# Relational attention with four heads at a time: scores in four row strips, relation sums in four column strips, one set of 8 PSUM banks

## Chip, cores, metric

The kernel runs on one core of one Trainium2 chip. The time is microseconds on the device, the median of several runs (they agree within 0.1%). The profile is one execution seen by the hardware profiler. PE is the matmul engine, PEld its weight loads, DVE, ACT and POOL the other compute engines. A record is one instruction in the profile; an fp32 matmul of the program is two records. The granted clock is the share of PE's full clock that was let through to it. The chain is the work that ended last, followed back from the end of the run. A PSUM bank is one of eight buffers that PE writes its results to. The runs were taken on several chips; the kernel before, run beside each of them, took 7752.3 to 7752.8 us in all of them.

## The reference, cut to what matters

Two layers over 64 graphs of 256 nodes with 256 features, all in fp32. Layer 0 is a graph attention (twice) with a feed-forward. Layer 1 is the one that changes:

```python
q, k: (64, 8 heads, 256, 32)
scores = einsum('bhid,bhjd->bhij', q, k) / sqrt(32)
attn = softmax(scores, axis=-1)
for r in range(4):
    v_r = src @ Wv[r] + bv[r]                      # per head: 256 x 32
    out += einsum('bhij,bhjd->bhid', attn * (adj_matrix == r), v_r)
attn_out = out @ Wo + bo                           # then norm, feed-forward (gelu), norm
```

A head has 32 features: a score matmul fills 32 rows of PE's 128 x 128 array, a relation sum (32 output features, 128 nodes contracted) 32 columns.

## The kernel before

Two graphs are one group, 32 groups follow each other. In a group's attention the heads are worked off one by one, `weighted` two heads ahead of `applied`:

```python
def bank(name):
    return psum.tile([P, 512], F32, tag="g", name=name, bufs=3)
...
def weighted(b, h):                                   # softmax, i on the partitions
    hp = slice(a * DH, (a + 1) * DH)                  # a = h % 4: the head's strip
    ps = psum.tile([P, NB, N], F32, tag="s", bufs=2)
    for i in range(NB):
        nc.tensor.matmul(ps[:, i, :], q[hp, m, i0:i0 + P], k_[hp, m, ...])          # sp
    nc.vector.tensor_reduce(nm[:, 0, :], ps, AX.X, ALU.max)                          # hm
    nc.vector.tensor_scalar(nm[:, 0, :], nm[:, 0, :], -isd, None, op0=ALU.mult)
    for i in range(NB):
        nc.scalar.activation(e[:, i, :], ps[:, i, :], AF.Exp, bias=nm[:, 0, i:i + 1],
                             scale=isd, accum_out=nm[:, 1, i:i + 1])
    nc.vector.reciprocal(nm[:, 2, :], nm[:, 1, :])
    nc.gpsimd.tensor_mul(e, e, ...)

def applied(b, h, e, po):
    pt = psum.tile([P, NB * N], F32, tag="pt", bufs=2)
    ...                                               # 4 transposes of e into pt
    for r in range(NR):                               # the four masks: er
        nc.vector.scalar_tensor_tensor(er[:, r, :], aT[b], float(r), pt,
                                       op0=ALU.is_equal, op1=ALU.mult)
    for r in range(NR):
        for j in range(NB):
            nc.tensor.matmul(po[hp, m, :], v[...head h...], er[:, r, j * N:(j + 1) * N],
                             start=(r == 0 and j == 0), stop=(r == NR - 1 and j == NB - 1))
```

The eight PSUM banks are 3 (general), 2 (scores), 2 (transposes) and 1 (sums). A scheduler fixes each engine's order when the kernel is built.

## Time and profile before

| | before |
|---|---|
| time | 7752.3 us (7750.9 to 7753.7, 4 runs) |
| PE, DVE busy | 85%, 39% of the span |
| one group | 240.6 us, of it the attention loop 98.8 us |

"The loop" is always the stretch from a group's first score matmul to the start of its second output projection; "the rest" is what lies between two loops.

### The profile page before, as it was taken

How to read it: one execution, taken by the hardware profiler on the slowest of the kernel's cores; microseconds unless marked ns; L12 is line 12 of the kernel's file. 1: busy time of each engine (PE TensorE's matmuls, PEld its weight loads, DVE VectorE, ACT ScalarE, POOL GpSimd, SP SyncE). 2: the span in 40 equal slices, each digit the busy share in tenths (PEclk: the TensorE clock that was granted, in tenths of full speed). 3: DMA queues.
4: the chain of work that ended last, by engine and by line, in shares of the span. 5: the costliest groups of instructions: out<-in, count | busy, mean ns of one | idle time of the engine just before them, and what ended most of it. 6: DMA issues, size and time to landing. Idle time of an engine off the chain costs nothing.

```text
span 7751.0 us, 62264 instructions
## 1 busy us (share of the span) xinstructions
PE 6591.3 (85%) x24104; PEld 3643.6 (47%) x24104; DVE 2999.6 (39%) x6544; ACT 1505.7 (19%) x3968; POOL 1417.2 (18%) x1193
## 2 busy tenths in 40 slices
PE   7888888888888888888888888888898888988888
PEld 4444444444444444444444444444444444444444
DVE  3344433344333443334433343433434334343343
ACT  1121122211212112122111221112211122111221
POOL 1111111111111111111111211111111111111111
PEclk8999989999989999899998999989999899998999
DMA  2000000000000000000000000000000000000000
GB/s 61 9 9 6 3 9 9 9 6 3 9 9 9 6 3 9 9 9 6 3 9 8 9 6 3 9 9 9 9 1 9 9 9 9 1 8 9 3 3 3
DMA packets 63094, 62.85 MB, mean 8 GB/s; under 512 B 7248, under 2 KB 62160, under 8 KB 62800
## 3 DMA queue, kind: packets, MB, share of 16 engines
q1 hardware_dynamic: 33792, 33.56, 1.3%
q0 software_dynamic: 16896, 16.78, 0.9%
q10 hardware_dynamic: 12112, 8.54, 0.4%
q8 instruction: 191, 3.13, 0.2%
q14 instruction: 103, 0.84, 0.0%
HBM read 42.09 MB, written 16.78 MB: 8 GB/s over the span
## 4 chain that ended last, share of the span: by engine, by line
PE 67%; issue 13%; DVE 11%; POOL 5%; ACT 3%; ACTq 0%; DMA 0%; POOLq 0%; DVEq 0%
PE po L321 24%; PE sp L292 7%; PE h1p L250 7%; PE yfp L216 6%; PE vp L278 6%; PE pt L313 5%; PE qp L266 2%; PE ygp L216 2%; PE gTp L355 2%; DVE er L317 2%; PE yop L216 2%; POOL rs L232 2%; PE kp L266 1%; DVE s L198 1%; DVE s L199 1%
## 5 line engine op out<-in xcount | busy, mean ns | idle before, releaser
L321 PE MATMUL po<-er,v 128*32 128x256 f32 x8192 | 1923.9, 391 | 154.6 <-DVE er L317 154.6
L317 DVE SCALAR_TENSOR_TENSOR er<-aT,pt 128x512 f32<-128x512 f32 x2048 | 1316.7, 678 | 1181.9 <-PE pt L313 1181.9
L321 PEld LDWEIGHTS po<-er,v 128*32 128x32 f32 x8192 | 783.7, 112 | 1073.9 <-DVE er L317 256.2
L302 POOL TENSOR_TENSOR e<-e,hm 128x512 f32<-128x512 f32 x512 | 531.7, 1041 | 3032.7 <-DVE hm L301 2980.3
L299 ACT ACTIVATE e<-sp,hm 128x256 f32<-128x256 f32 x1024 | 476.0, 470 | 2625.0 <-DVE hm L296 2624.9
L219 DVE TENSOR_TENSOR yf<-yfp,res 128x512 f32<-128x512 f32 x128 | 88.5, 692 | 1770.1 <-PE yfp L216 1770.1
L292 PE MATMUL sp<-k,q 32*128 32x256 f32 x2048 | 649.3, 429 | 67.4 <-ACT e L299 67.4
L250 PE MATMUL h1p<-h1T,wf 128*128 128x512 f32 x1024 | 519.0, 671 | 23.8 <-DVE h1T L153 23.8
L250 PE MATMUL h1p<-h3T,w 128*128 128x512 f32 x1024 | 515.6, 668 | 22.1 <-DVE h3T L153 22.1
L292 PEld LDWEIGHTS sp<-k,q 32*128 32x128 f32 x2048 | 304.0, 189 | 360.2 <-issue 266.6
L216 PE MATMUL yfp<-w,h 128*128 128x256 f32 x2048 | 447.3, 379 | 0.0
L216 PE MATMUL yfp<-wf,h 128*128 128x256 f32 x2048 | 447.2, 379 | 0.0
L278 PE MATMUL vp<-wv,h2T 128*128 128x512 f32 x1024 | 444.7, 592 | 0.0
L313 PE MATMUL pt<-ident,e 128*128 128x128 f32 x2048 | 418.9, 307 | 7.3 <-POOL e L302 6.3
L232 POOL TENSOR_TENSOR rs<-ve,mhalf 128x4 f32<-128x4 f32 x128 | 130.7, 1021 | 1588.3 <-DVE ve L231 1588.3
L216 PEld LDWEIGHTS yfp<-w,h 128*128 128x128 f32 x2048 | 389.1, 190 | 66.6 <-issue 15.3
L216 PEld LDWEIGHTS yfp<-wf,h 128*128 128x128 f32 x2048 | 389.1, 190 | 66.6 <-issue 15.3
L280 DVE TENSOR_TENSOR v<-vp,rbv 128x512 f32<-128x512 f32 x256 | 177.1, 692 | 561.9 <-PE vp L278 561.9
L313 PEld LDWEIGHTS pt<-ident,e 128*128 128x128 f32 x2048 | 223.2, 146 | 325.4 <-issue 271.1
L250 PEld LDWEIGHTS h1p<-h1T,wf 128*128 128x128 f32 x1024 | 219.5, 218 | 306.9 <-issue 256.5
L250 PEld LDWEIGHTS h1p<-h3T,w 128*128 128x128 f32 x1024 | 218.3, 217 | 305.7 <-issue 254.3
L295 DVE TENSOR_REDUCE hm<-sp 128x2 f32<-128x512 f32 x512 | 350.0, 684 | 14.9 <-PE sp L292 11.7
(470 smaller groups left out, 5798.8 us busy)
## 6 DMA issues: line engine op xcount, KB each, us to landing
xs<-in_x_dram SPq DMA_DIRECT2D x32, 512.0 KB, 3.5
af<-in_adj_dram POOLq DMA_DIRECT2D x32, 512.0 KB, 4.2
out_dram<-res SPq DMA_DIRECT2D x32, 512.0 KB, 2.8
wf<-in_L_gnn_w_ff_dram ACTq DMA_DIRECT2D x2, 1024.0 KB, 12.4
w<-in_L_gnn_W_dram ACTq DMA_DIRECT2D x2, 1024.0 KB, 9.9
wv<-in_L_gnn_Wv_dram ACTq DMA_DIRECT2D x4, 256.0 KB, 5.1
rbv<-in_L_gnn_bv_dram ACTq DMA_DIRECT2D x1, 512.0 KB, 6.8
gat1we<-in_L_gnn_W_dram ACTq DMA_DIRECT2D x1, 256.0 KB, 4.2
```

What stands on the lines that cost most here:

```text
L216: nc.tensor.matmul(ps[:, i * F:(i + 1) * F], lhs(t, k), rhs(b, k), start=(k == 0), stop=(k == n - 1))
L232: nc.gpsimd.tensor_tensor(rs, ve, mhalf, ALU.pow)
L250: nc.tensor.matmul(ps, wi[:, k, f * P:(f + 1) * P], hT[:, k, :], start=(k == 0), stop=(k == KB - 1))
L266: nc.tensor.matmul(ps, w[:, k, m * P:(m + 1) * P], hT[:, k, :], start=(k == 0), stop=(k == KB - 1))
L278: nc.tensor.matmul(ps, hT[:, k, t * P:(t + 1) * P], wvf[:, k, cs], start=(k == 0), stop=(k == KB - 1))
L292: nc.tensor.matmul(ps[:, i, :], q[hp, m, i0:i0 + P], k_[hp, m, b * N:(b + 1) * N], start=True, stop=True)
L295: nc.vector.tensor_reduce(nm[:, 0, :], ps, AX.X, ALU.max)
L299: nc.scalar.activation(e[:, i, :], ps[:, i, :], AF.Exp, bias=nm[:, 0, i:i + 1], scale=isd, accum_out=nm[:, 1, i:i + 1])
L302: nc.gpsimd.tensor_mul(e, e, nm[:, 2, :, None].to_broadcast([P, NB, N]))
L313: nc.tensor.transpose(pt[:, j * N + i * P:j * N + (i + 1) * P], e[:, i, j * P:(j + 1) * P], ident)
L317: nc.vector.scalar_tensor_tensor(er[:, r, :], aT[b], float(r), pt, op0=ALU.is_equal, op1=ALU.mult)
L321: nc.tensor.matmul(po[hp, m, :], v[:, b * NB + j, r * F + h * DH:r * F + (h + 1) * DH], er[:, r, j * N:(j + 1) * N], start=(r == 0 and j = ...
```

## The change

The intent: four heads of a feature block (a "quad") lie in four different strips of the array, so if their matmuls alternate, PE can run four at once. The core of the diff:

```diff
-        def weighted(b, h):
-            ps = psum.tile([P, NB, N], F32, tag="s", name=f"sp{n}", bufs=2)
+        def weighted(b, m):
+            ps = [bank(f"sp{n}_{a}") for a in range(HPB)]
             for i in range(NB):
-                nc.tensor.matmul(ps[:, i, :], q[hp, m, i0:i0 + P], ...)
+                for a in range(HPB):
+                    hp = slice(a * DH, (a + 1) * DH)
+                    nc.tensor.matmul(ps[a][:, i * N:(i + 1) * N], q[hp, m, i0:i0 + P], ...)
+            for a in range(HPB):
+                ...                                   # softmax as before, head by head
-        def applied(b, h, e, po):
-            pt = psum.tile([P, NB * N], F32, tag="pt", name=f"pt{n}", bufs=2)
+        def applied(b, m, es, po):
+            for a in range(HPB):
+                pt = bank(f"pt{n}_{a}")
+                ...                                   # transposes and masks, head by head
             for r in range(NR):
                 for j in range(NB):
-                    nc.tensor.matmul(po[hp, m, :], ...)
+                    for a in range(HPB):              # heads innermost
+                        nc.tensor.matmul(po[hp, m, :], ...)
-        ahead = [weighted(*heads[0]), weighted(*heads[1])]
+        ahead = [weighted(*quads[0])]                 # one quad ahead
```

With it, `bank` becomes one set of `bufs=8` for everything; the masks `er` get five buffers (before: two), which the feed-forward's hidden layer, cut in two halves, shares; the exponentials `e` get five (before: three); three other buffers are reduced by one to make room. DVE, ACT and POOL have the same instructions as before.

More of the change, by code (lines that the diff above doesn't have):

```diff
@@ L54, in bank @@
     def bank(name):
-        return psum.tile([P, 512], F32, tag="g", name=name, bufs=3)
+        return psum.tile([P, 512], F32, tag="g", name=name, bufs=8)
     def load(u):
@@ L98, in gat_weights @@
         nc.vector.tensor_copy(ar, ac[:, :, None].to_broadcast([P, 2 * KB, P]))
-        wt = work.tile([P, KB, F], F32, tag="h1", name=f"{name}wt", bufs=1)
+        wt = work.tile([P, KB, F], F32, tag="big", name=f"{name}wt", bufs=5)
         for c in range(KB):
@@ L143, in to_features @@
     def to_features(src, name, scale=None, shift=None):
-        dst = work.tile([P, KB, TN], F32, tag="hT", name=name, bufs=3)
+        dst = work.tile([P, KB, TN], F32, tag="hT", name=name, bufs=2)
         for k in range(KB):
@@ L179, in gat_weighted @@
             nc.tensor.matmul(rows, wa[:, k, :], hT[:, k, :], start=(k == 0), stop=(k == KB - 1))
-        wh = work.tile([P, T, F + 1], F32, tag="wh", name=f"wh{name}")
+        wh = work.tile([P, T, F + 1], F32, tag="wh", name=f"wh{name}", bufs=1)
         for t in range(T):
@@ L186, in gat_weighted @@
             nc.scalar.copy(wh[:, t, :], ps[:, :F + 1])
-        s = work.tile([P, T, N], F32, tag="s", name=f"s{name}")
+        s = work.tile([P, T, N], F32, tag="s", name=f"s{name}", bufs=1)
         for t in range(T):
@@ L245, in feed_forward @@
     def feed_forward(u, l, hT, wi, bi, func, wo_, res):
-        h1 = work.tile([P, FB, TN], F32, tag="h1", name=f"h1{u}_{l}", bufs=1)
+        h1 = [work.tile([P, FB // 2, TN], F32, tag="big", name=f"h1{u}_{l}_{c}", bufs=5)
+              for c in range(2)]
         for f in range(FB):
@@ L251, in feed_forward @@
                                  start=(k == 0), stop=(k == KB - 1))
-            nc.scalar.activation(h1[:, f, :], ps, func, bias=bi[:, f:f + 1])
+            nc.scalar.activation(h1[f * 2 // FB][:, f % (FB // 2), :], ps, func, bias=bi[:, f:f + 1])
         y = work.tile([P, T, F], F32, tag="y", name=f"yf{u}_{l}")
         for b in range(G):
-            add_blocks(u, f"yfp{l}_", y, res, b, lambda t, k: h1[:, k, t * P:(t + 1) * P],
+            add_blocks(u, f"yfp{l}_", y, res, b, lambda t, k: h1[k * 2 // FB][:, k % (FB // 2), t * P:(t + 1) * P],
                        lambda b, k: wo_[:, k, :], FB)
@@ L282, in attention @@
         isd = 1.0 / math.sqrt(DH)
-        def weighted(b, h):
-            m, a = divmod(h, HPB)
-            hp = slice(a * DH, (a + 1) * DH)
-            n = f"{u}_{b}_{h}"
-            ps = psum.tile([P, NB, N], F32, tag="s", name=f"sp{n}", bufs=2)
+        def weighted(b, m):
+            n = f"{u}_{b}_{m}"
+            ps = [bank(f"sp{n}_{a}") for a in range(HPB)]
             for i in range(NB):
                 i0 = b * N + i * P
-                nc.tensor.matmul(ps[:, i, :], q[hp, m, i0:i0 + P],
-                                 k_[hp, m, b * N:(b + 1) * N], start=True, stop=True)
-            nm = work.tile([P, 3, NB], F32, tag="hm", name=f"hm{n}", bufs=4)
-            nc.vector.tensor_reduce(nm[:, 0, :], ps, AX.X, ALU.max)
-            nc.vector.tensor_scalar(nm[:, 0, :], nm[:, 0, :], -isd, None, op0=ALU.mult)
-            e = work.tile([P, NB, N], F32, tag="e", name=f"e{n}", bufs=3)
-            for i in range(NB):
-                nc.scalar.activation(e[:, i, :], ps[:, i, :], AF.Exp, bias=nm[:, 0, i:i + 1],
-                                     scale=isd, accum_out=nm[:, 1, i:i + 1])
-            nc.vector.reciprocal(nm[:, 2, :], nm[:, 1, :])
-            nc.gpsimd.tensor_mul(e, e, nm[:, 2, :, None].to_broadcast([P, NB, N]))
-            return e
@@ L305, in applied @@
-        def applied(b, h, e, po):
-            m, a = divmod(h, HPB)
-            hp = slice(a * DH, (a + 1) * DH)
-            n = f"{u}_{b}_{h}"
-            pt = psum.tile([P, NB * N], F32, tag="pt", name=f"pt{n}", bufs=2)
-            for j in range(NB):
-                for i in range(NB):
-                    nc.tensor.transpose(pt[:, j * N + i * P:j * N + (i + 1) * P],
-                                        e[:, i, j * P:(j + 1) * P], ident)
-            er = work.tile([P, NR, NB * N], F32, tag="er", name=f"er{n}", bufs=2)
-            for r in range(NR):
-                nc.vector.scalar_tensor_tensor(er[:, r, :], aT[b], float(r), pt,
-                                               op0=ALU.is_equal, op1=ALU.mult)
+                for a in range(HPB):
+                    hp = slice(a * DH, (a + 1) * DH)
+                    nc.tensor.matmul(ps[a][:, i * N:(i + 1) * N], q[hp, m, i0:i0 + P],
+                                     k_[hp, m, b * N:(b + 1) * N], start=True, stop=True)
@@ new lines, in weighted @@
+            nm = work.tile([P, HPB, 3, NB], F32, tag="hm", name=f"hm{n}", bufs=3)
+            es = []
+            for a in range(HPB):
+                pv = ps[a].rearrange("p (i n) -> p i n", i=NB)
+                nc.vector.tensor_reduce(nm[:, a, 0, :], pv, AX.X, ALU.max)
+                nc.vector.tensor_scalar(nm[:, a, 0, :], nm[:, a, 0, :], -isd, None, op0=ALU.mult)
+                e = work.tile([P, NB, N], F32, tag="e", name=f"e{n}_{a}", bufs=5)
+                for i in range(NB):
+                    nc.scalar.activation(e[:, i, :], pv[:, i, :], AF.Exp, bias=nm[:, a, 0, i:i + 1],
+                                         scale=isd, accum_out=nm[:, a, 1, i:i + 1])
+                nc.vector.reciprocal(nm[:, a, 2, :], nm[:, a, 1, :])
+                nc.gpsimd.tensor_mul(e, e, nm[:, a, 2, :, None].to_broadcast([P, NB, N]))
+                es.append(e)
@@ new lines, in weighted @@
+            return es
+        def applied(b, m, es, po):
+            n = f"{u}_{b}_{m}"
+            ers = []
+            for a in range(HPB):
+                pt = bank(f"pt{n}_{a}")
+                for j in range(NB):
+                    for i in range(NB):
+                        nc.tensor.transpose(pt[:, j * N + i * P:j * N + (i + 1) * P],
+                                            es[a][:, i, j * P:(j + 1) * P], ident)
+                er = work.tile([P, NR, NB * N], F32, tag="big", name=f"er{n}_{a}", bufs=5)
+                for r in range(NR):
+                    nc.vector.scalar_tensor_tensor(er[:, r, :], aT[b], float(r), pt,
+                                                   op0=ALU.is_equal, op1=ALU.mult)
+                ers.append(er)
@@ L319, in applied @@
             for r in range(NR):
                 for j in range(NB):
-                    nc.tensor.matmul(po[hp, m, :],
-                                     v[:, b * NB + j, r * F + h * DH:r * F + (h + 1) * DH],
-                                     er[:, r, j * N:(j + 1) * N],
-                                     start=(r == 0 and j == 0),
-                                     stop=(r == NR - 1 and j == NB - 1))
-        heads = [(b, h) for b in range(G) for h in range(H)]
-        ahead = [weighted(*heads[0]), weighted(*heads[1])]
@@ L329, in attention @@
-        for n, (b, h) in enumerate(heads):
-            if h == 0:
-                po = psum.tile([P, KB, N], F32, tag="o", name=f"po{u}_{b}")
-            applied(b, h, ahead.pop(0), po)
-            if n + 2 < len(heads):
-                ahead.append(weighted(*heads[n + 2]))
-            if h == H - 1:
+                    for a in range(HPB):
+                        h = m * HPB + a
+                        hp = slice(a * DH, (a + 1) * DH)
+                        nc.tensor.matmul(po[hp, m, :],
+                                         v[:, b * NB + j, r * F + h * DH:r * F + (h + 1) * DH],
+                                         ers[a][:, r, j * N:(j + 1) * N],
+                                         start=(r == 0 and j == 0),
+                                         stop=(r == NR - 1 and j == NB - 1))
@@ L336, in attention @@
+        quads = [(b, m) for b in range(G) for m in range(KB)]
+        ahead = [weighted(*quads[0])]
+        for n, (b, m) in enumerate(quads):
+            if n + 1 < len(quads):
+                ahead.append(weighted(*quads[n + 1]))
+            if m == 0:
+                po = bank(f"po{u}_{b}").rearrange("p (m n) -> p m n", m=KB)
+            applied(b, m, ahead.pop(0), po)
+            if m == KB - 1:
                 nc.scalar.copy(oT[:, :, b * N:(b + 1) * N], po)
@@ L348, in tile_gat_layer__then__relational_attention_layer @@
         att, whs = gat_weighted(u, 0, hT, gat1, off)
-        hT = work.tile([P, KB, TN], F32, tag="hT", name=f"gT{u}", bufs=3)
+        hT = work.tile([P, KB, TN], F32, tag="hT", name=f"gT{u}", bufs=2)
         for m in range(KB):
```

## The prediction

> **What bounds the kernel now.** I read the page's busy table first (PE 85% of the span, DVE 39%), then the chain that ended last (PE 67%, its largest line the relation sums `po`), then the groups, and then one of the 32 groups of two graphs as a timeline. In the chain the second feed-forward of a group starts at 2416.89 us and that of two groups later at 2898.13 us: 240.6 us a group, and x 32 that is 7700 of the 7751 us. The kernel is 32 equal copies, laid end to end. Inside a group the attention loop runs from the first score matmul at 2310.08 us to the second output projection at 2408.90 us. These are busy times by engine in that stretch, and the chain in it:
>
> ```profile
> 2310.08:2408.90 98.82, 90.67 (x394) 42.29 (x393) 55.08 (x118) 17.45 (x67) 16.61 (x16) 0.97 0.00 1
> ```
>
> The columns are length, then PE, weight load, DVE, ACT and POOL busy, then the granted clock. The loop is 98.8 us, 41% of a group, and PE is busy in 90.7 of it at nearly full clock; DVE in 55.1. The rest of the group (142 us) is not touched by the change except for buffer counts. The groups that the change concerns:
>
> ```profile
> L321 PE MATMUL po<-er,v 128*32 128x256 f32 x8192 | 1923.9, 391 | 154.6 <-DVE er L317 154.6
> L317 DVE SCALAR_TENSOR_TENSOR er<-aT,pt 128x512 f32<-128x512 f32 x2048 | 1316.7, 678 | 1181.9 <-PE pt L313 1181.9
> ...
> L292 PE MATMUL sp<-k,q 32*128 32x256 f32 x2048 | 649.3, 429 | 67.4 <-ACT e L299 67.4
> ...
> L313 PE MATMUL pt<-ident,e 128*128 128x128 f32 x2048 | 418.9, 307 | 7.3 <-POOL e L302 6.3
> ...
> L295 DVE TENSOR_REDUCE hm<-sp 128x2 f32<-128x512 f32 x512 | 350.0, 684 | 14.9 <-PE sp L292 11.7
> ```
>
> The reader is to see that `po` uses 32 of 128 columns and `sp` 32 of 128 rows, that each fp32 matmul of the program is two records (64 graphs x 8 heads x 2 score products make x2048 records, x 8 relation products x8192), and that DVE waited 1181.9 us for the transposes: it follows PE. The means of 391 and 429 ns are latencies of pipelined work; start to start, single records say otherwise: `po` 213 ns (most of its intervals lie at 210 to 219), `sp` 213, `pt` 108. So a loop of 16 heads needs on PE 256 x 0.213 = 54.5 us for `po`, 64 x 0.213 = 13.6 for `sp`, 64 x 0.108 = 6.9 for `pt`: 75 us. The other 24 us are changes between the three shapes (a first record after a change starts 307 ns after the last, against 213: some 0.1 us, five or six times a head, 9 us), the lead-in, and 6.8 us at half clock near the start.
>
> **Do strips overlap?** Already now, where two heads meet by accident:
>
> ```profile
> 2310.08 1.14 PE L292 MATMUL sp<-k,q 32*128 32x256 f32 x8
> ...
> 2377.10 1.93 PE L321 MATMUL po<-er,v 128*32 128x256 f32 x12
> 2378.96 0.69 PE L292 MATMUL sp<-k,q 32*128 32x256 f32 x2
> ```
>
> Eight score records of heads 0 and 1 take 1.14 us; one after the other they would need 8 x 0.213 + 0.2 of tail = 1.9. In single records the two heads start 13 ns apart and then each keeps its 213 ns pace, although the program has all of head 0 first. Twelve `po` records take 1.93 us, where 12 x 0.213 + 0.2 is 2.76: four pairs, 13 ns apart. So row strips and column strips both run side by side in fp32, for two. Four at once are in no trace here.
>
> **What the Trainium skill says.** "TensorEngine Tiling (Array Packing)", Key Properties: different tiles load weights and multiply in parallel, and a change of tiling mode drains the array; the trace agrees with both (13 ns apart; 307 against 213 ns). "TensorE: Matmul & The Clock Gate", Part 3, gives 3.07x measured for four row tiles and 2.38x for three column tiles; the trace has only the pairs. The tiling page again, PSUM Bottleneck: tiling speeds up the array and not the reading of its results, which may then bound; here DVE's 55.1 us in the 98.8 is that second limit. The clock page, Part 1: the array's clock falls to half after a window of 3.4 us with too little work. The trace has it: after 2.1 us of idle PE at the loop's start the clock is 0.5 from 2315.9 to 2322.7 us and 1.0 for the next 92 us.
>
> **The change, part by part.**
>
> 1. *Relation sums*, heads innermost, four column strips. 54.5 us become 13.6 if four run together (16 records a strip and quad, 3.4 us a quad).
> 2. *Scores*, four row strips: 13.6 become 3.4. Transposes are unchanged, 6.9. Changes of shape fall from about 90 to about 50 in a loop, say 5 us. PE: 13.6 + 3.4 + 6.9 + 5 = 29 us, no longer the bound.
> 3. *DVE* has the same instructions. From the trace: the four masks of a head start 598 ns apart (four span 2.48 us), 64 x 0.598 = 38.3 us; a reduce of 0.60 to 0.69, 16 of them 10.3; 32 small ones that cost 0.08 to 0.17 each, 4. Together about 53 us; the measured 55.1 less the 1.7 of a norm's first half that lay in the loop is 53.3. I take 53.3 as the new floor.
> 4. *Lead-in.* In the changed order DVE does the reduces of quads 0 and 1, and stands at a reciprocal of quad 1's first head before the first mask. That needs five heads' exponentials, 0.92 us each (two of 128x256 start 0.46 apart), 4.6 us after the first negated maximum at +2: the first mask starts at about +7, of which DVE has filled some 5. With 1.2 us before the first reduce and 1 us where the next three reciprocals wait at ACT's pace, I count 3.5 us lost.
> 5. *Between quads.* Order of PE: next scores and the next quad's first two transposes stand ahead of the block of `po`. The block starts with the last head's first mask and runs 3.4 us; DVE needs 1.8 for the other three masks, so PE ends about 1.5 us behind. Meanwhile DVE has reduces (2.9 us) and a fifth mask buffer (2.4 us), so it should not stand for the four buffers of the quad. I allow 0.5 us a quad at ACT's pace, 1.5 in all.
> 6. *Tail.* Last block 1.5 us behind DVE, drain 0.3, copy of `po` 0.7: 2.7 us before the output projection.
> 7. *Clock.* PE works 29 of 62 us, so half clock some of the time. A block of `po` is then 6.9 us, against 7.1 of DVE work that does not need its buffers; the cost is mostly the tail. I allow 1.5 us.
>
> Sum: 53.3 + 3.5 + 1.5 + 2.7 + 1.5 = 62.5 us for a loop, 36.3 less than 98.8; 32 x 36.3 = 1162 us. The 8 banks in one set, and the single buffers of the graph attention's scores, should do nothing: outside the loop every matmul that could run ahead waits for data, and the orders there are the same. 7753 - 1162 = **6590 us**, a ratio of 0.85.
>
> **The rivals.**
>
> *Four column strips do not overlap as pairs do.* At two together `po` is 27 us, PE 43, still below DVE: nothing changes but the tail, +2 us a loop, 6650. With no overlap PE has 54.5 + 3.4 + 6.9 + 3 = 68, with lead-in 74 us a loop: 6960. The pairs in the trace speak against it.
>
> *The clock gate.* If it stays at half through the loop, PE needs nearly 58 us, and each block ends late enough to stop DVE for 2 to 3 us; the projection and the next layer start cold as well. 72 us a loop, 6890. The one cold stretch now came in a window where PE was busy by half, so this is the likeliest way for me to be too low.
>
> *Lockstep.* Four heads share five mask buffers and eight banks. If DVE stood through each block and the transposes after it (3.4 + 4 us) a quad would be 20 us, a loop 85, and the time 7310. The built order speaks against it; a wait that I overlooked would show here.
>
> *A better outcome.* DVE never stands after the lead-in and the clock is full: 53.3 + 4 = 57 us, 6415.
>
> **Range and chances.** 57 us a loop gives 6415 and 70 gives 6830, with the clock rival nearly inside; I say 6400 to 6850. Slower than 7600 needs over 94 us a loop, which none of these reach; I leave a little for what I have not seen.
>
> **What would show it.** Right: the loop at 60 to 65 us in the windows, DVE busy over 80% of it, PE under half at full clock; `po` records four at a time within some 40 ns, each strip at 213 ns; the chain's `po` share from 24% down to 5 to 8% and the masks' up to 20% or more; the rest of a group at 142 us within 2. Step 1 wrong: blocks of 64 `po` records over 5 us at full clock. Step 5 wrong: masks waiting for `po` over 1 us a quad. Step 7 wrong: a granted clock below 0.7 in the loop, and a rest of the group that grew. The prediction as a whole is wrong if DVE is not the engine that sets the loop.

## The result and the profile after

The changed kernel takes 6495.0 us (6493.3 to 6496.3, 4 runs), a ratio of 0.838 (0.837 to 0.839). The prediction was 6590, range 6400 to 6850.

The same loop, in the same view as before (length; busy PE, weight load, DVE, ACT, POOL; granted clock):

```profile
2155.18:2213.86 58.68, 44.89 (x394) 23.70 (x393) 53.46 (x118) 16.36 (x67) 16.19 (x16) 0.88 0.00 1
```

40.1 us of the loop are gone (mean of 32 loops: 98.8 to 58.7). DVE, with the same 118 instructions, is now busy in 53.5 of 58.7 us. The chain that ended last and the groups of the page say the same:

```profile
PE 46%; DVE 27%; issue 17%; ACT 5%; POOL 5%; ACTq 0%; DMA 0%; POOLq 0%; DVEq 0%
...
L322 DVE SCALAR_TENSOR_TENSOR er<-aT,pt 128x512 f32<-128x512 f32 x2048 | 1253.8, 677 | 0.0
L330 PE MATMUL po<-er,v 128*32 128x256 f32 x8192 | 814.2, 458 | 150.7 <-DVE er L322 149.6
```

PE's share of the chain fell from 67% to 46%, DVE's rose from 11% to 27%. The masks, which waited 1181.9 us for the transposes, now wait for nothing. The sums' busy time fell from 1923.9 to 814.2 us because more of them lie over each other. The mean of one rose from 391 to 458 ns because more run at half clock: a record takes 379 ns at full clock and 634 at half, and 30% of them, against 4% before, took over 450. One loop's end in the timeline of PE:

```profile
2197.40 3.65 PE L330 MATMUL po<-er,v 128*32 128x256 f32 x60
2202.18 0.62 PE L330 MATMUL po<-er,v 128*32 128x256 f32 x2 [1.14 <-DVE er L322]
2204.57 0.62 PE L330 MATMUL po<-er,v 128*32 128x256 f32 x2 [1.77 <-DVE er L322]
2206.96 6.22 PE L330 MATMUL po<-er,v 128*32 128x256 f32 x58 [1.77 <-DVE er L322]
2213.86 1.99 PE L216 MATMUL yop<-wo,oT 128*128 128x256 f32 x8 [0.68 <-ACT oT L345]
```

The first line is the third quad's block: 60 records in 3.65 us, against 13.0 us one after the other at 0.216. In single records four start within 20 ns (0, 7, 13, 20 ns), the next four 240 ns after them, and from then on four every 216 ns: fourfold overlap, in fp32, in column strips. The fourth line is the last quad's block, nearly the same work (58 records) in 6.22 us: the trace's clock record says 0.5 from 2205.4 to 2212.2 us. The changes of the clock near it (2174.68, 2205.40, 2212.22 us) lie multiples of 3.41 us apart. In the window of 3.4 us before the clock fell, PE was busy for 1.24 us, and around it PE waits 1.77 us for masks twice. So the loop now ends with PE at half speed, and nothing overlaps that: the output projection needs the last sum.

From the single records of all loops, the mean of when, counted from the loop's start, the first mask starts and the last one ends, what follows the last mask up to the projection (the tail), and how long the clock is at half:

| kernel | us | loop | first mask | last mask ends | tail | half clock in the loop | rest |
|---|---|---|---|---|---|---|---|
| before | 7752 | 98.8 | 5.4 | 96.2 | 2.6 | 6.8 | 141.8 |
| changed | 6495 | 58.7 | 8.1 | 53.5 | 5.1 | 13.9 | 142.7 |

This table is continued below for the experiments.

### The profile page after: what moved, and what is told of

The parts are those of the page before. It is cut to its first block, busy times and chain, and to the rows that moved or that the text cites. A ratio compares the mean times of both kernels' runs of the same rounds, so it can differ in the third digit from the quotient of the medians.

```text
span 6494.2 us, 62227 instructions
## 1 busy us (share of the span) xinstructions
PE 5157.5 (79%) x24104; PEld 3084.4 (47%) x24104; DVE 2940.3 (45%) x6544; ACT 1452.8 (22%) x3968; POOL 1403.8 (22%) x1193
## 4 chain that ended last, share of the span: by engine, by line
PE 46%; DVE 27%; issue 17%; ACT 5%; POOL 5%; ACTq 0%; DMA 0%; POOLq 0%; DVEq 0%
DVE er L322 13%; PE h1p L251 8%; PE po L330 7%; PE yfp L216 7%; PE vp L279 7%; PE gTp L364 3%; PE qp L267 3%; PE ygp L216 3%; DVE hm L299 2%; ACT e L303 2%; POOL rs L232 2%; PE kp L267 2%; DVE s L198 2%; DVE s L199 2%; PE rows L179 1%
## 5 line engine op out<-in xcount | busy, mean ns | idle before, releaser
L322 DVE SCALAR_TENSOR_TENSOR er<-aT,pt 128x512 f32<-128x512 f32 x2048 | 1253.8, 677 | 0.0
L330 PE MATMUL po<-er,v 128*32 128x256 f32 x8192 | 814.2, 458 | 150.7 <-DVE er L322 149.6
L306 POOL TENSOR_TENSOR e<-e,hm 128x512 f32<-128x512 f32 x512 | 518.3, 1042 | 1350.0 <-DVE hm L300 1043.6
L330 PEld LDWEIGHTS po<-er,v 128*32 128x32 f32 x8192 | 337.8, 131 | 545.8 <-DVE er L322 252.7
L318 PE MATMUL pt<-ident,e 128*128 128x128 f32 x2048 | 377.1, 315 | 267.1 <-POOL e L306 160.2
L251 PE MATMUL h1p<-h1T,wf 128*128 128x512 f32 x1024 | 496.6, 647 | 22.1 <-DVE h1T L153 22.1
L318 PEld LDWEIGHTS pt<-ident,e 128*128 128x128 f32 x2048 | 243.8, 155 | 447.2 <-POOL e L306 244.2
L364 PE MATMUL gTp<-s,wh 128*128 128x256 f32 x512 | 213.9, 606 | 238.0 <-POOL wh L206 238.0
L253 ACT ACTIVATE h<-h1p,bf 128x512 f32<-128x512 f32 x256 | 176.0, 687 | 778.2 <-PE h1p L251 778.2
L216 PE MATMUL ygp<-wh,s 128*128 128x256 f32 x512 | 206.9, 590 | 177.8 <-POOL wh L206 177.8
## 6 DMA issues: line engine op xcount, KB each, us to landing
w<-in_L_gnn_W_dram ACTq DMA_DIRECT2D x2, 1024.0 KB, 10.9
```

The source lines that it names most:

```text
L216: nc.tensor.matmul(ps[:, i * F:(i + 1) * F], lhs(t, k), rhs(b, k), start=(k == 0), stop=(k == n - 1))
L251: nc.tensor.matmul(ps, wi[:, k, f * P:(f + 1) * P], hT[:, k, :], start=(k == 0), stop=(k == KB - 1))
L306: nc.gpsimd.tensor_mul(e, e, nm[:, a, 2, :, None].to_broadcast([P, NB, N]))
L318: nc.tensor.transpose(pt[:, j * N + i * P:j * N + (i + 1) * P], es[a][:, i, j * P:(j + 1) * P], ident)
L330: nc.tensor.matmul(po[hp, m, :], v[:, b * NB + j, r * F + h * DH:r * F + (h + 1) * DH], ers[a][:, r, j * N:(j + 1) * N], start=(r == 0 and ...
L364: nc.tensor.matmul(ps[:, b * N:(b + 1) * N], whs[:, t, m * P:(m + 1) * P], att[:, t, :], start=(j == 0), stop=(j == NB - 1))
```

## The experiments

All were built from the changed kernel except two from the kernel before; all gave the right result.

### 1. Heads outermost again

```diff
-            for r in range(NR):
-                for j in range(NB):
-                    for a in range(HPB):
+            for a in range(HPB):
+                for r in range(NR):
+                    for j in range(NB):
                         nc.tensor.matmul(po[hp, m, :], ...)
```

> The changed kernel with the relation sums of a quad written head by head (head outermost) and all else kept. Theory 1: strips run together only when their matmuls alternate in the program; then PE needs 54.5 us for the sums, about 69 in all, and a loop is about 73 us: 6950 us. Theory 2: the array starts the next strip as soon as its data and the queue allow, as two heads did by accident in the kernel before; PE then falls behind DVE only until strips overlap, a loop stays under 65 us and the time under 6700 us. In its trace: single starts of po less than 40 ns apart are few under theory 1, many under theory 2.

Measured: 7151.3 us (ratio 0.922), 200 us over what theory 1 expected, a loop of 80.1 us (not 73) with PE busy in 74.4 of it. This is its chain in one loop:

```profile
by line: PE po L330 64.8%; PE pt L318 11.2%; PE sp L293 10.8%; PE yop L216 3.5%; DVE hm L299 3.1%; POOL e L306 2.6%; ACT e L303 1.3%; issue 1.0%; ACT oT L345 0.8%; DVE er L322 0.7%; PE vp L279 0.5%; DVE hm L300 0.5%; DVE hm L305 0.3%; ACTq 
```

PE sets this loop again. Only 896 of 8192 sums start within 40 ns of the one before; in the changed kernel 5440 do. The mechanism of theory 1 holds: the array does start another strip out of turn, but too seldom to live from it; the alternation in the program is needed. It is worth 656 us, just over half of the gain. The other 601 us are there with heads outermost: the scores four at a time, fewer stretches of one shape on PE (82 a loop before, 45 here), the banks. The two traces say where that time went. Counted from one PE start to the next, idle time apart, the scores take 9.5 us of a loop here and 18.8 before, the sums 52.0 and 57.9, the transposes 10.9 and 11.8, and PE is idle for 5.4 and 8.1. So about half of the 601 us lies in the scores. What shapes, clock and banks have in each part, no run separates beyond experiment 8.

### 2. Blocks of two heads

```diff
+            for a0 in range(0, HPB, 2):
                 for r in range(NR):
                     for j in range(NB):
-                        for a in range(HPB):
+                        for a in range(a0, a0 + 2):
```

> The changed kernel with the relation sums of a quad in two blocks of two heads (strips 0 and 1, then 2 and 3), all else kept. Theory 1: DVE sets the loop and PE's clock costs nothing but the tail; half the overlap then changes nothing: 6495 us within 0.5%, and the sums take twice the PE time. Theory 2: the fuller PE keeps its clock at full, so that the last block of a loop takes 3.4 us and not 6.2 and the feed-forward starts warm: 3 to 5 us a loop less, 6330 to 6400 us. Theory 3: four at once is what the gain rests on: over 6600 us.

Measured: 6392.2 us (ratio 0.8245), 1.6% faster than four at a time and in theory 2's range. The last block of a loop, and the loop:

```profile
2177.28 3.64 PE L331 MATMUL po<-er,v 128*32 128x256 f32 x30 [1.14 <-DVE er L322]
...
2124.26:2181.60 57.34, 49.74 (x394) 29.11 (x393) 53.46 (x118) 16.12 (x67) 16.21 (x16) 0.97 0.00 1
```

A strip has 16 records in either kernel; at full clock they take 3.64 us, at half 6.22. Half clock in the loop falls from 13.9 to 3.6 us, the tail from 5.1 to 2.6, the rest from 142.7 to 140.8. Against this, the last mask ends 1.3 us later.

### 3. Four mask buffers for five

(The same number stands at two other users of these buffers.)

```diff
-                er = work.tile([P, NR, NB * N], F32, tag="big", ..., bufs=5)
+                er = work.tile([P, NR, NB * N], F32, tag="big", ..., bufs=4)
```

> The changed kernel with four mask buffers in place of five. Theory 1: the fifth buffer is what lets DVE go on while PE works off a block; without it DVE stands 1 us at the first and 2 to 3 us at the last change of quad, 2 to 4 us a loop: 6560 to 6620 us. Rival (lockstep): the scheduler then can place nothing ahead of a block, DVE stands for block and transposes, over 8 us a loop: over 6750 us.

Measured: 6501.0 us, 0.1% over the changed kernel. Both theories expected more. The loop is 1.0 us longer and the rest 0.9 us shorter. DVE's timeline shows one wait of 0.47 us for the sums between the first two quads and none between the next; before the last masks the scheduler has put the first projection's addition and norm, 1.7 us of work, where I had DVE standing. The fifth buffer is worth next to nothing here.

### 4. No maximum in the softmax

```diff
-                nc.vector.tensor_reduce(nm[:, a, 0, :], pv, AX.X, ALU.max)
-                nc.vector.tensor_scalar(nm[:, a, 0, :], nm[:, a, 0, :], -isd, None, op0=ALU.mult)
-                    nc.scalar.activation(..., AF.Exp, bias=nm[:, a, 0, i:i + 1], scale=isd, ...)
+                    nc.scalar.activation(..., AF.Exp, scale=isd, ...)
```

> The changed kernel without the maximum of the softmax (no reduce, no negation; the exponentials take the plain scores, which are small here, so the result should stay right). Theory 1: DVE sets the loop now; it loses 16 x 0.68 us, the first mask comes at about +6 us in place of +8: a loop of about 50 us, 6200 us (6150 to 6280). Rival: PE or its chain of waits sets the loop; then under 1% is gained, over 6430 us.

Measured: 6274.9 us (ratio 0.809), 3.4% under the changed kernel and in the range expected; the loop is 52.4 us, though, not 50. One loop:

```profile
2082.18:2134.67 52.49, 43.43 (x393) 23.39 (x392) 42.32 (x86) 13.75 (x67) 16.09 (x16) 0.84 0.00 1
```

DVE's masks now end at 48.0 us, for which DVE is busy about 41: it no longer sets the whole loop, and the half clock grew to 17.1 us.

### 5. The sums of two heads computed twice

```diff
+            for r in range(NR):                       # thrown away: the block starts anew
+                for j in range(NB):
+                    for a in range(2):
+                        nc.tensor.matmul(po[hp, m, :], ..., start=(r == 0 and j == 0), ...)
             for r in range(NR):
                 for j in range(NB):
                     for a in range(HPB):
```

> The changed kernel, but the relation sums of heads 0 and 1 of a quad are computed once more ahead of the block of four, and thrown away (the block starts its sums anew): strictly more work for PE, 13.6 us a loop at full clock, and the last block of four as long as in the changed kernel. Theory 1 (clock): what made pairs faster is only that PE has work while DVE makes the last masks of a loop, so its clock is full when the last block and the feed-forward come. Then this is as fast as pairs, 6380 to 6430 us, with a granted clock above 0.95 in the loop. Theory 2 (shape of the blocks): pairs gained because half of the sums were done early; then the added work gains nothing, 6490 us or more.

Measured: 6444.8 us (ratio 0.831): with half as many sums again, it is 0.8% *faster* than the changed kernel. The last block of a loop, again a block of four, and the loop:

```profile
2191.53 3.64 PE L340 MATMUL po<-er,v 128*32 128x256 f32 x58 [0.51 <-DVE er L322]
...
2137.62:2195.84 58.22, 51.92 (x521) 29.76 (x520) 53.63 (x118) 16.25 (x67) 16.19 (x16) 0.97 0.01 1
```

6.22 us became 3.64 with the same instructions in the block; the tail is 2.6 us as in pairs, and the rest 141.2. So the clock, and not the shape of the blocks, made that end slow. Theory 2, that the added work gains nothing, has fallen. The time is not that of pairs, and over theory 1's range: the last mask ends at 56.0 us, in pairs at 54.8 and in the changed kernel at 53.5. POOL and PE are on the chain earlier in the loop, so the added work probably stands in the way there; that was not tested.

### 6. Both savings

> Both savings together: no maximum, and the sums in two blocks of two. Theory: the one takes work off DVE (190 us less in the first of 32 loops times 6 us each), the other keeps PE's clock; a loop falls from 52.4 to about 50 us and the rest of a group from 142 to 140.8: 6140 to 6180 us. Rival: with less time for the same PE work the clock is full without pairs, then 6270 us.

(The bracket in the text means 32 loops with 6 us less in each.) Measured: 6277.9 us, the same as without pairs. The rival's number is near, but not for its reason: without pairs the granted clock of the loop is 0.84, not full. The tail fell to 2.6 us, but the last mask moved from 48.0 to 50.8 us. Without the maximum, DVE has less to do, and the doubled PE time of pairs probably gets in its way (the chain of the loop holds the sums at 32%, against 22%).

### 7. The kernel before, without the maximum

> The kernel before without the maximum. Theory: PE sets its loop, so the same cut that gave the changed kernel 220 us gives this one only a shorter lead-in, about 1 us a loop: 7700 to 7752 us. Rival: DVE's work lies on the path in the kernel before as well: under 7600 us.

Measured: 7480.4 us (ratio 0.965). The theory has fallen: the cut gives the kernel before 272 us, more than the 220 of the changed one. Its loop:

```profile
2231.96:2321.03 89.07, 86.44 (x393) 41.66 (x392) 43.10 (x86) 14.43 (x67) 16.53 (x16) 1.00 0.00 1
```

The clock is 1.00: the 6.8 us at half near the start are gone. The first sum comes 5.2 us after the loop's start and not 8.4, PE is idle for 2.6 us of the loop and not 8.1, and there are 72 stretches of one shape, not 82. The rest of a group grew from 141.8 to 143.0 us. PE is still the bound (86.4 of 89.1 us). With these, a gain from DVE's cut is no proof that DVE sets a loop: a shorter lead-in also moves the clock and the order. Their shares were not separated by a run.

### 8. The kernel before with one set of 8 banks

```diff
-        return psum.tile([P, 512], F32, tag="g", name=name, bufs=3)
+        return psum.tile([P, 512], F32, tag="g", name=name, bufs=8)
-            ps = psum.tile([P, NB, N], F32, tag="s", name=f"sp{n}", bufs=2)
+            ps = bank(f"sp{n}").rearrange("p (i n) -> p i n", i=NB)      # pt, po alike
```

> The kernel before with its 3 + 2 + 2 + 1 PSUM banks in one set of 8, one head at a time as before. Theory: the banks are not what PE waits for; 7752 us within 1%. Rival: the set of banks is part of the gain: under 7600 us.

Measured: 7585.2 us (ratio 0.978). The theory has fallen, and the rival holds: one set of banks alone is worth 167 us to the kernel before. One loop:

```profile
2257.25:2350.25 93.00, 87.34 (x393) 43.53 (x392) 55.34 (x118) 17.45 (x67) 16.61 (x16) 0.98 0.00 1
```

The loop is 93.0 us, with 67 stretches of one shape in place of 82, 3.4 us at half clock in place of 6.8, and the first sum at 6.0 us in place of 8.4. I had looked at the banks only outside the loop.

### 9. Blocks of two in the last quad alone

```diff
+            last = b == G - 1 and m == KB - 1
+            for hs in ((0, 1), (2, 3)) if last else ((0, 1, 2, 3),):
                 for r in range(NR):
                     for j in range(NB):
-                        for a in range(HPB):
+                        for a in hs:
```

> The changed kernel with blocks of two for the last quad of a loop alone, blocks of four elsewhere. Theory (clock at the end of the loop): a tail of 2.6 us as in pairs in place of 5.1, the masks ending at 53.5 us as with fours, and a rest of 140.8 us as in pairs: 4.5 us a group less, 6350 us (6330 to 6380), faster than pairs. Rival (the clock needs a full PE through the whole loop, or the gain is in the other quads): 6450 us or more.

Measured: 6386.8 us (ratio 0.824). The loop is 56.1 us, which is 53.5 + 2.6 as expected; the rest is 141.9 and not 140.8, so that the time is 37 us over the middle of what I expected, outside its range, and no clear gain on pairs (0.1%). The end of the loop:

```profile
2166.03 3.64 PE L332 MATMUL po<-er,v 128*32 128x256 f32 x32 [1.14 <-DVE er L322]
2170.82 3.64 PE L332 MATMUL po<-er,v 128*32 128x256 f32 x30 [1.14 <-DVE er L322]
```

The block of the first two heads fills the time in which PE had waited; the second runs at full clock. What the rest takes does not follow from the loop's end alone: here its mean clock is 0.869, as in the changed kernel, and in pairs 0.889.

### 10. The best version: last quad in pairs, no maximum

> The same without the maximum. Without it, blocks of two everywhere moved the last mask from 48.0 to 50.8 us and ate the shorter tail; blocks of two in the last quad alone should keep 48.5 us and have the tail of 2.6: loop 51, rest 141, 192 us a group: 6200 us (6170 to 6230). Rival: the last quad's pairs delay its masks as well, then 6275 us.

Measured: 6168.6 us (ratio 0.796), 5.0% faster than the changed kernel and the fastest of all. The loop is 50.4 us, last mask at 48.0, tail 2.6, rest 140.7: all as expected, with the time just under the range. One loop:

```profile
2048.79:2099.33 50.54, 43.45 (x393) 24.08 (x392) 42.31 (x86) 13.77 (x67) 16.10 (x16) 0.90 0.00 1
```

It is right for these inputs, where scores are small; leaving out the maximum would not be safe for scores of any size. Experiment 9 is the best one that keeps it.

### 11. The changed kernel with its banks split

```diff
-        return psum.tile([P, 512], F32, tag="g", name=name, bufs=8)
+        return psum.tile([P, 512], F32, tag="g", name=name, bufs=4)
-                pt = bank(f"pt{n}_{a}")
+                pt = psum.tile([P, NB * N], F32, tag="pt", name=f"pt{n}_{a}", bufs=3)   # po: 1
```

> The changed kernel with its 8 banks split again: 4 for scores and all else, 3 for transposes, 1 for the sums. The one set gave the kernel before 167 us. Theory: there it gave PE's order fewer changes of shape and an earlier start; here PE has slack and DVE sets the loop, so it is within 1% of 6495 us. Rival: with four heads in flight the set matters more; over 6620 us.

Measured: 6509.6 us, 0.2% over the changed kernel: the theory holds. The first mask comes at 10.2 us in place of 8.1 and the last ends at 56.5 in place of 53.5, but the last block then meets a full clock and the tail is 2.8. So the 0.2% is a difference of two larger effects.

The table again, means over the loops of each profile (the first loop or two differ; leaving them out moves a figure by up to 0.4 us):

| kernel | us | loop | first mask | last mask ends | tail | half clock in the loop | rest |
|---|---|---|---|---|---|---|---|
| heads outermost | 7151 | 80.1 | 8.1 | 70.1 | 10.0 | 4.1 | 141.8 |
| pairs | 6392 | 57.4 | 8.1 | 54.8 | 2.6 | 3.6 | 140.8 |
| two heads twice | 6445 | 58.6 | 8.1 | 56.0 | 2.6 | 5.5 | 141.2 |
| last quad in pairs | 6387 | 56.1 | 8.1 | 53.5 | 2.6 | 7.1 | 141.9 |
| no maximum | 6275 | 52.4 | 5.0 | 48.0 | 4.5 | 17.1 | 142.1 |
| no maximum, last quad in pairs | 6169 | 50.4 | 5.0 | 48.0 | 2.6 | 10.2 | 140.7 |

## Why the prediction was right, point by point

- **The gain sits in the loop, and DVE takes over as its bound: right.** DVE is busy in 53.5 of 58.7 us, the masks wait for nothing, and half as many sums again (experiment 5) or twice the PE time for them (experiment 2) do not lengthen the kernel. The Trainium skill, "TensorEngine Tiling (Array Packing)", PSUM Bottleneck, warns that reading the results may become the bound, and it did: DVE is busy in 53.5 of 58.7 us. What DVE reads, though, are the scores and the transposes, not the sums.
- **Steps 1 and 2, overlap: right.** Four records start within 20 ns and each strip keeps 216 ns; a block is 3.6 us at full clock, 3.4 by my count plus the tail of the last record. My 213 ns was slightly misread: in the kernel before, most intervals between sums are 215 or 216 ns. The pairs seen by accident in the kernel before were a sound ground for it. Stretches of one shape fell to 26 a loop, not 50. For the scores my count of the kernel before was too low: the two records of a score matmul that stands alone start 320 ns apart, and PE spent 18.8 us a loop on scores, not 13.6; afterwards it spends 6.9, not 3.4.
- **Step 3, DVE's floor of 53.3 us: a little high.** DVE's 53.5 busy us include the 1.7 of the norm in both kernels; without it 51.7. Twelve masks in a row take 7.24 us, 0.60 each as counted. Their mean duration is unchanged (678 and 677 ns), but their busy time fell from 1316.7 to 1253.8 us: in longer runs more of them overlap.
- **Steps 4 and 5, waits of 5 us: too high.** The last mask ends at 53.5 us, 1.8 us over DVE's own work. The first mask came at 8.1 us and not 7, but DVE had reduces and reciprocals to do until then: I counted that time as lost, and it was not. With four buffers (experiment 3) hardly more is lost.
- **Steps 6 and 7, tail and clock, 2.7 + 1.5 us: too low by 0.9 us, and the clock weighed more than I said.** The tail is 2.6 us at full clock (experiments 2, 5, 9) and 5.1 in the changed kernel. The rest of a group grew by 0.9 us besides, where I had allowed none.
- **Sum.** Of the loop I had 3.8 us too much and of the rest 0.9 too little: 32 x 2.9 = 93 us, which is the distance from 6590 to 6495. Part of this closeness is luck: steps 3 to 5 were about 4.8 us too high, and the tail and the rest 1.8 too low.
- **The rivals.** Lockstep did not come, and strips overlapped. The clock gate was right in kind, 13.9 us at half in a loop, but mostly hidden under DVE's work; the 2.5 us at the end of each loop are its price inside it.
- **What was to show it.** PE under half busy did not come (44.9 of 58.7 us; the records' own length counts in that), and the masks have 13% of the chain, not 20%. DVE as a whole has 27%. The sums fell from 24% to 7% of it, as expected.
- **The banks "should do nothing": right for the changed kernel (0.2%), wrong for the kernel before (2.2%).** The bank set did next to nothing beside the four heads, and something without them. For the changed kernel it was right in part by luck: splitting the banks makes the last mask 3.0 us later, and the shorter tail makes up for most of it (experiment 11).

Open: what shapes, lead-in, clock and banks each have in the 601 us that come without the alternation of the sums (about half of it lies in the scores, experiment 1); and why the rest of a group is 140.7 us in some kernels and 142.7 in others, beyond the observation that its mean clock differs (0.889 and 0.868 in pairs and in the changed kernel).

## What to carry to other kernels

Matmuls that use a quarter of the array ran four at a time here, in fp32, once their strips alternated in the program; look in the old trace for two that already do so by accident. Once PE is off the path, its clock is part of the plan: work that comes early and keeps it busy can be worth more than the tightest packing, above all just ahead of a stretch where the next step waits for PE. And a cut on an engine that is not the bound may still pay through the lead-in, so such a cut alone proves no bound.

## What the Trainium skill lacked or had wrong

- "TensorE: Matmul & The Clock Gate", Part 3, says that matmuls start strictly in program order. Across strips they do not here, by the starts in the profile: in the kernel before, the built program has all score matmuls of head 0 ahead of those of head 1, and the records of the two alternate, 13 ns apart, each head at its own pace.
- The same part gives 3.07x for four row tiles and 2.38x for three column tiles, and nothing for four column tiles. In a full block of this kernel's fp32 sums four column strips keep the pace of one: four records every 216 ns, 60 in 3.65 us against 13.0.
- The same page, Part 1, names an idle window as what halves the clock; the prediction's "too little work" is wider than that. Here it also fell after windows of 3.4 us in which PE was busy for 2.4 us (before, up to 2315.9 us, with scores of one strip and transposes) and 1.24 us (after, up to 2205.4 us). Which of this work counts for the clock, no run here separates.
- "TensorEngine Tiling (Array Packing)", Key Properties, says that a change of tiling mode drains the array, without a size. Here the first record after a sum or a score, when the shape changes, starts 304 to 310 ns after it and not 216. From a transpose to a projection matmul, both of the whole array, it is 109 ns as between transposes.
